# A sixth block's layer ahead of the second MLP's turn, an output evicted amid the gates' choice, and the experts' weights split sooner

## Chip, core and metric

The kernel runs on one core of one Trainium2 chip. The metric is the device time of one execution in microseconds (us); lower is better. Times of single instructions come from one profiled execution and are counted from the start of its span.

## What is computed

The reference is one block of a gated cross-attention model on `x` of 16 x 256 tokens with 256 features. Cut to what matters:

```
ref_xattn(z, x):
  zn    = layernorm(z @ W_in + b_in)                  # 16 x 120 context tokens
  h     = silu(pe @ Wp1 + bp1) @ Wp2 + bp2            # a filter, times a window
  dcwhz = causal_convolution(zn, window * h)[every second step]
  xr    = x + silu(layernorm(x) @ W1a + b1a) @ W1b + b1b        # first MLP
  y     = xr * dcwhz
  return y + silu(layernorm(y) @ W2a + b2a) @ W2b + b2b         # second MLP

ref_ffn(x):                                            # 8 heads of 32, 16 experts, 2 chosen
  t      = (x @ Wm + bm) split into heads of 32
  w      = softmax(t @ expert_emb); top two of 16, lowest index first on ties
  hmid   = gelu(t @ W1[e] + b1[e])                     # all 16 experts, 128 wide
  eo     = hmid @ W2[e] + b2[e]
  return (sum over the chosen of w * eo) @ Wo + bo

x = x + tanh(g_xattn) * ref_xattn(ctx, layernorm(x))
x = x + tanh(g_ffn)   * ref_ffn(layernorm(x))
```

The output is 4096 rows of 256 in float32. The kernel gets its accuracy by splitting most matmul operands in a high and a low part and adding three products (hi x hi, lo x hi, hi x lo).

## The kernel before

The 4096 tokens are cut in eight blocks of 512 (`NB`, `TB`). A block is a job of three kinds: `Mlp1` (first MLP, `jobs[0..7]`), `Mlp2` (second MLP, `mlp20`, `mlp21`, `mlps[2..7]`) and `Route` (choice of the experts, `route0`, `routes[1..7]`). Each job has the same steps. `norms` finds the roots of the variances on VectorE (ten tiny instructions, lines 146 to 165, and an offset, L175). `prep` normalises (L184 on ScalarE, L188 on VectorE). `turn` transposes on TensorE (L235), copies the high part out of PSUM on ScalarE (L237) and the low part on VectorE (L238). `first` is a layer with four groups of six matmuls (L205), each followed by two ScalarE activations (L259, L260) and a subtraction on VectorE or GpSimd (L268). `second` is a layer of 48 matmuls (L278), and its output is evicted by VectorE (L884 for the first MLP, L361 for the second, followed there by the statistics L170 and L171).

The program has three stages. In the first some 157 us the first MLP's blocks 0 to 4 are interleaved with the convolution. Then comes the stage that the change touches, "behind the convolution", from 157 us to some 250 us. There blocks 5 to 7 of the first MLP, blocks 0 and 1 of the second MLP and the choice of block 0 are brought up to the point where the third stage can begin. The third stage is a loop of 256 steps, one for each block, half of the heads and expert. A step has four matmuls `hps` (L1273), two Gelu activations on ScalarE (L1278), four matmuls `eo` (L1288), a VectorE product with the gates (L1296) and a GpSimd sum (L1298). The remaining MLPs and choices ride along in the loop at steps that `begun` names (`layer`, `split_laid`, `heads`, `logits`).

From line 965 on, the order of the instructions on each engine is the order in which the Python code issues them (`tc.manual_schedule()`); nothing reorders them. Generators are what interleaves work: `whole(gen)` issues all that is left of a job's step, `some(gen, n)` the next n pieces of it. Each engine takes its queue in order, so an instruction that waits holds up everything behind it on that engine, and SyncE's DMA queue is likewise in order.

Buffers set further waits. PSUM has the pools `turn`, `first`, `second` and `conv`, two banks each; `last_bank` hands out those of `conv`. `first` on a third group needs the bank of the first group back, and so the ScalarE activations that read it. `second` needs two banks at once. The staging tiles of the late weights (`stage`) have two buffers.

`late_weights` is a generator that loads and splits the weights of the third stage. `halves` splits one weight in two parts, the high part on ScalarE (L999) and the low part on GpSimd (L1000). Before the change it goes: load `Wm` and the embeddings; split them; load both halves of the experts' `W1` and `b1`, and `W2`; split both halves of `W1` (L1048 on ScalarE, L1049 on GpSimd); load `Wo`; split `Wo`. `some(weights)` at certain places of the stage takes one step of it.

`choose` is the gates' choice on VectorE: transpose (L436), maximum (L449), difference (L452), exponential on ScalarE (L458), sum and reciprocal (L461, L463), a GpSimd product (L464), then a chain of eight compare and reduce steps (L468 to L481), two GpSimd products (L482, L483) and a transpose (L488). It yields after most steps, and the loop over `route0.second(last_bank)` puts a piece of `behind_it()` after each.

Of the kernel before, what the change touches and what calls it, by code (L numbers as in the profile page):

```python
# [24 lines left out]
FP = mybir.dt.float32  # L25
# [8 lines left out]
P = 128  # L34
# [59 lines left out]
def block_kernel(  # L94
# [445 lines left out]
    with ExitStack() as ph:  # L540
# [476 lines left out]
        def late_weights():  # L1017


            t_wm = staged(Wm.rearrange("(c p) n -> p c n", p=P), 2, D, nc.sync)  # L1020
            t = first_p.tile([P, 4 * D], FP, name="stage", tag="stage", bufs=2)
            t = t.rearrange("p (q c) -> p q c", c=P)[:, 0:2]
            nc.gpsimd.memset(t, 0.0)
            for q in range(2):
                for g in range(4):
                    nc.sync.dma_start(t[bass.ts(g, HD), q, bass.ts(4 * q + g, E)], emb)
            yield
            halves(wm, t_wm)
            halves(bd, t)
            yield  # L1030
            ts = []
            for q in range(2):
                ee = slice(8 * q, 8 * q + 8)
                t = first_p.tile([P, 4 * D], FP, name="stage", tag="stage", bufs=2)
                t = t.rearrange("p (e i) -> p e i", i=I)[0:KST]
                for g in range(3):
                    nc.sync.dma_start(t[bass.ts(g, HD)], W1[ee].rearrange("e h i -> h e i"))
                for k in range(2):
                    nc.sync.dma_start(
                        t[3 * HD + k : 3 * HD + k + 1], b1[ee].unsqueeze(0)  # L1040
                    )
                ts.append((wst[0:KST, ee], t))
            nc.sync.dma_start(w2s, W2.rearrange("e i o -> i e o"))
            yield

            low = slice(2 * HD, 3 * HD + 1)
            for w, t in ts:
                nc.scalar.copy(w, t)  # L1048
                nc.gpsimd.tensor_tensor(w[low], t[low], w[low].bitcast(FP), ALU.subtract)  # L1049
            yield  # L1050
            t = staged(Wo.rearrange("(c p) n -> p c n", p=P), 2, D, nc.sync)
            yield
            halves(wo, t)
            yield
# [85 lines left out]
        jobs[5].prep()  # L1140
        some(weights)
        whole(turn(mlp20, last_bank, place))
        whole(turn(jobs[5], bank))
        some(weights)
        ahead = jobs[5].first(bank)
        mlp21.stats()
        whole(mlp20.first(last_bank))
        mlps[2].stats()
        some(ahead, 2)
        mlp21.norms(mlps[2])  # L1150
# [3 lines left out]
        for t in stacks[:2]:  # L1154
            units(t)
        whole(ahead)
        route0.norms()
# [23 lines left out]
        def behind_it():  # L1181
# [4 lines left out]
            yield from mlp21.second(bank)  # L1186
            yield from jobs[6].first(bank)
            free.append(place)
# [6 lines left out]
            lay(a)  # L1195
            some(weights)
            yield
# [8 lines left out]
            nc.scalar.activation(gelu, cv[:, 0:1], AF.Gelu)  # L1206
            some(weights)
            for _ in jobs[7].second(bank):
# [13 lines left out]
        for n, _ in enumerate(route0.second(last_bank)):  # L1222
            if n == 0:
                load_stacks(0, route0.td)
                some(rest)
            some(rest)
        while not free:
# [11 lines left out]
    with ExitStack() as ph:  # L1239
# [389 lines left out]
```

## Time and profile before

| | |
|---|---|
| median of 3 runs | 937.1 us (934.39 to 937.55) |
| profiled execution, whole time | 936.37 us |
| its span, first to last instruction | 934.6 us |
| TensorE (PE) busy | 897.2 us, 96% of the span |
| VectorE (DVE) busy | 707.2 us, 76% |
| ScalarE (ACT) busy | 673.2 us, 72% |
| GpSimd (POOL) busy | 565.6 us, 61% |
| 157 to 250 us: PE, DVE, ACT, POOL busy | 85.5, 70.6, 62.7, 47.9 of 93.0 us |
| mean granted TensorE clock | 0.987 |

Busy shares are averages over stages with different limits, so a change in one stage is read from that stage's own waits. "PEld" is the loading of weights, which lies beside the matmuls. "PEclk" is the share of the TensorE clock that was granted in a stretch: 1.00 is full speed, 0.50 half. A row of a timeline gives start, duration, engine, line, operation, tiles and shape, and in brackets the idle time of the engine before it and what ended that.

### The profile page before, as it was taken

The page shows a single profiled execution, that of the slowest core. Times are in us where ns is not written, and L with a number is a line of the kernel's source. Part 1 is how long each engine was busy: PE and PEld are TensorE (multiplying, and loading weights), DVE is VectorE, ACT ScalarE, POOL GpSimd, SP SyncE. Part 2 cuts the span into 40 slices and gives each one's busy share as a digit, 9 for nine tenths or more (in the row PEclk, how much of TensorE's full clock was granted, in tenths as well). Part 3 has the DMA queues.
Part 4 walks back from the last instruction along what each step waited for, and adds up shares of the span by engine and source line. Part 5 has one row for each costly group of instructions (what it writes and reads, how often), then busy time and mean ns, then how long its engine had stood idle before and what let it go on. Part 6 is the DMA issues. An engine that isn't in the chain of part 4 may idle for free.

```text
span 934.6 us, 16793 instructions
## 1 busy us (share of the span) xinstructions
PE 897.2 (96%) x6070; PEld 485.9 (52%) x6070; DVE 707.2 (76%) x1304; ACT 673.2 (72%) x862; POOL 565.6 (61%) x456
## 2 busy tenths in 40 slices
PE   5999998999889999999999999999999999989996
PEld 2777777887434445444454445444545434433333
DVE  5886548776778988998799789879985984783343
ACT  3544445686678788778778887887787777877883
POOL 4222123446568767777777867777767757585553
PEclk9999999999899999999999999999999999999997
DMA  7668970444439466846765694678566756836441
GB/s 244 171 201 219 217 175 24 94 114 124 135 99 228 127 175 191 196 141 160 216 162 141 186 235 118 168 198 198 151 163 191 166 141 169 215 94 177 124 124 46
DMA packets 88296, 149.89 MB, mean 160 GB/s; under 512 B 10250, under 2 KB 51722, under 8 KB 88206
## 3 DMA queue, kind: packets, MB, share of 16 engines
q1 hardware_dynamic: 85428, 141.08, 57.6%
q0 software_dynamic: 1808, 6.69, 2.3%
q10 hardware_dynamic: 976, 1.05, 0.4%
q8 instruction: 48, 0.79, 0.4%
q14 instruction: 36, 0.29, 0.1%
HBM read 120.32 MB, written 28.46 MB: 159 GB/s over the span
## 4 chain that ended last, share of the span: by engine, by line
PE 60%; DVE 20%; DMA 8%; issue 6%; POOL 2%; ACT 2%; SPq 2%; POOLq 0%; DVEq 0%; ACTq 0%
PE hps L1273 19%; PE eo L1288 17%; DVE part L1296 5%; PE aux L1332 5%; DMA gates<-g_d 4%; PE b_first L205 4%; PE b_second L278 3%; PE b_conv L908 2%; PE aux L205 2%; DMA hk<-filt_d 2%; DMA t_d<-t_lo 1%; PE b_conv L205 1%; DVE ex L371 1%; DVE d L481 1%; PE b_conv L724 1%
## 5 line engine op out<-in xcount | busy, mean ns | idle before, releaser
L1278 ACT ACTIVATE hid<-hps 128x1024 f32<-128x1024 f32 x512 | 512.4, 1026 | 139.6 <-PE hps L1273 126.1
L1298 POOL TENSOR_TENSOR comb<-comb,part 128x512 f32<-128x512 f32 x240 | 329.7, 1374 | 159.7 <-DVE part L1296 154.0
L1273 PE MATMUL hps<-stack,wst 98*128 98x512 f32 x1024 | 342.4, 426 | 4.6 <-ACT hid L1278 4.6
L1273 PEld LDWEIGHTS hps<-stack,wst 98*128 98x128 f32 x1024 | 162.9, 189 | 249.7 <-ACT hid L1278 120.0
L1288 PE MATMUL eo<-hid,w2s 128*32 128x512 f32 x2048 | 274.1, 607 | 7.8 <-DVE part L1296 7.3
L1296 DVE SCALAR_TENSOR_TENSOR part<-eo,cv,gates 128x512 f32<-128x512 f32 x237 | 175.5, 744 | 90.6 <-PE eo L1288 68.2
L1288 PEld LDWEIGHTS eo<-hid,w2s 128*32 128x32 f32 x2048 | 40.6, 108 | 102.9 <-issue 47.2
L268 POOL TENSOR_TENSOR s_lo<-silu,s_hi 128x512 fp32r<-128x512 f32 x16 | 20.4, 1287 | 68.5 <-ACT silu L260 54.8
L1391 POOL TENSOR_TENSOR s_lo<-silu,s_hi 128x512 fp32r<-128x512 f32 x24 | 31.0, 1293 | 33.6 <-DVE s_hi L1390 27.0
L1389 DVE SCALAR_TENSOR_TENSOR silu<-silu,u 128x512 f32<-128x512 f32 x24 | 26.1, 1086 | 22.6 <-ACT u L1386 22.6
L1423 DVE TENSOR_SCALAR n<-Y,mv,r_r 128x256 f32<-128x256 f32 x44 | 37.2, 887 | 3.0 <-POOL nt_lo L1447 3.0
L259 ACT ACTIVATE s_hi<-b_first,b1f 128x512 fp32r<-128x512 f32 x32 | 22.0, 686 | 22.5 <-PE b_first L205 21.8
L278 PE MATMUL b_second<-v_hi,s_hi 128*128 128x256 f32 x144 | 37.3, 292 | 0.0
L278 PE MATMUL b_second<-v_lo,s_hi 128*128 128x256 f32 x144 | 36.0, 283 | 0.0
L1447 POOL TENSOR_TENSOR nt_lo<-n,nt_hi 128x512 fp32r<-128x512 f32 x26 | 33.6, 1292 | 3.0 <-PE hps L1273 2.6
L908 PE MATMUL b_conv<-hk,zn 60*32 60x256 f32 x1024 | 31.8, 378 | 0.0
L915 ACT COPY cvs<-b_conv 128x256 f32<-128x256 f32 x32 | 10.5, 375 | 27.5 <-PE b_conv L908 27.4
L278 PEld LDWEIGHTS b_second<-v_hi,s_hi 128*128 128x128 f32 x144 | 27.6, 191 | 3.3 <-issue 2.8
L1446 DVE CAST nt_hi<-n 128x512 fp32r<-128x512 f32 x26 | 28.2, 1084 | 0.0
L1471 POOL TENSOR_TENSOR Y<-Y,tbo 128x256 f32<-128x256 f32 x28 | 28.0, 1011 | 0.0
L278 PEld LDWEIGHTS b_second<-v_lo,s_hi 128*128 128x128 f32 x144 | 27.6, 192 | 0.4
L205 PE MATMUL b_first<-nt_hi,w_hi 128*128 128x512 f32 x64 | 27.2, 426 | 0.6 <-ACT silu L260 0.6
(284 smaller groups left out, 1480.2 us busy)
## 6 DMA issues: line engine op xcount, KB each, us to landing
gates<-g_d SPq DMA_DIRECT2D x126, 512.0 KB
hk<-filt_d SPq DMA_DIRECT2D x128, 134.1 KB
stack<-t_d SPq DMA_DIRECT2D x48, 256.0 KB
g_d<-gt SPq DMA_DIRECT2D x32, 256.0 KB
n<-laid_d SPq DMA_DIRECT2D x13, 512.0 KB
laid_d<-laid SPq DMA_DIRECT2D x44, 128.0 KB
xr<-in_x SPq DMA_DIRECT2D x8, 512.0 KB
t_d<-t_hi SPq DMA_DIRECT2D x16, 256.0 KB
```

Of the source, the lines that this page charges most:

```text
L205: nc.tensor.matmul(out=out, lhsT=l, rhs=r, start=(i == 0 and j == 0), stop=(i == n - 1 and j == 2),)
L278: nc.tensor.matmul(out=ps[:, j, :], lhsT=s[k][l][:, c], rhs=v[r][:, k], start=(k == 0 and i == 0 and not (whole and (j or bias))), stop=(k ...
L908: nc.tensor.matmul(out=ps[bass.ts(c, 2 * B), 0:L], lhsT=zn[rows, 4 * n + c, k, e * B : (e + 2) * B], rhs=hk[rows, 2 * c + e, k * SQ : k * ...
L1273: nc.tensor.matmul(out=ps[:, g, :], lhsT=wst[0:KST, e, :], rhs=st[0:KST, 2 * g2 + g, :], start=True, stop=True,)
L1278: nc.scalar.activation(t, ps, AF.Gelu)
L1288: nc.tensor.matmul(out=eo[bass.ts(g, HD)], lhsT=w2s[:, e, :], rhs=hid[g // 2][:, g % 2, :], start=True, stop=True,)
L1296: nc.vector.scalar_tensor_tensor(to, eo, col("b2", e), gs, ALU.add, ALU.mult)
L1298: nc.gpsimd.tensor_tensor(comb, comb, to, ALU.add)
L1332: nc.tensor.matmul(out=ps, lhsT=w[l][:, k, c], rhs=r[:, k], start=(k == 0 and j == 0), stop=(k == 1 and j == 2),)
L1391: nc.gpsimd.tensor_tensor(lo, f, hi.bitcast(FP), ALU.subtract)
L1423: nc.vector.tensor_scalar(job.n[:, j + k, :], Y[:, t0 + k, :], mv[:, t0 + k, 0:1], job.r[:, j + k : j + k + 1], ALU.subtract, ALU.mult,)
L1447: nc.gpsimd.tensor_tensor(lo, src, hi.bitcast(FP), ALU.subtract)
```

## The change

It moves work within the stage behind the convolution and shifts some pieces of the loop's first block; no arithmetic is added or removed.

1. **The sixth block's layer.** `turn(jobs[5])` and the first two groups of `jobs[5].first` are issued ahead of `turn(mlp20)`. Before, both turns came first, and these two groups stood between `mlp20.first` and `mlp20.second`.
2. **Weights.** `Wo` is loaded together with the first half of the experts' `W1`, in place of the second half, and split in the middle of the stage. The second half of `W1` is loaded after that. The first half of `W1` is split between the second and third group of `jobs[6].first`, the second half after `jobs[7].first`. The splits at the stage's end go away.
3. **The output amid the choice.** After each of the first three yields of `route0.second` one more piece of `behind_it()` is issued (three, two and two in place of two, one and one). The eviction of `mlp21.second` (L361, with its statistics) so comes after the fifth compare step (L472) and not after the last (L481).
4. **The loop's first block.** The pieces of `layer(m)` go from steps 2, 2, 3, 3, 4, 4, 5, 5 to 2, 3, 4, 4, 5, 5, 6, 7; `split_laid(a)`, `heads` and `logits` come one step later.

```diff
@@ late_weights
-            ts = []
-            for q in range(2):
+            def experts(q):
...
-                ts.append((wst[0:KST, ee], t))
-            nc.sync.dma_start(w2s, W2.rearrange("e i o -> i e o"))
-            yield
-
-            low = slice(2 * HD, 3 * HD + 1)
-            for w, t in ts:
+                return wst[0:KST, ee], t
+
+            def experts_split(w, t):
+
+                low = slice(2 * HD, 3 * HD + 1)
                 nc.scalar.copy(w, t)
                 nc.gpsimd.tensor_tensor(w[low], t[low], w[low].bitcast(FP), ALU.subtract)
-            yield
-            t = staged(Wo.rearrange("(c p) n -> p c n", p=P), 2, D, nc.sync)
-            yield
-            halves(wo, t)
+
+            t_wo = staged(Wo.rearrange("(c p) n -> p c n", p=P), 2, D, nc.sync)
+            some_experts = experts(0)
+            nc.sync.dma_start(w2s, W2.rearrange("e i o -> i e o"))
+            yield
+            halves(wo, t_wo)
+            t = experts(1)
+            yield
+            experts_split(*some_experts)
+            yield
+            experts_split(*t)
             yield
@@ behind the convolution
         some(weights)
+        whole(turn(jobs[5], bank))
+        ahead = jobs[5].first(bank)
+        some(ahead, 2)
         whole(turn(mlp20, last_bank, place))
-        whole(turn(jobs[5], bank))
         some(weights)
-        ahead = jobs[5].first(bank)
         mlp21.stats()
         whole(mlp20.first(last_bank))
         mlps[2].stats()
-        some(ahead, 2)
...
         for t in stacks[:2]:
             units(t)
+        some(weights)
         whole(ahead)
@@ behind_it
-            yield from jobs[6].first(bank)
+            soon = jobs[6].first(bank)
+            for n, _ in enumerate(soon):
+                if n == 1:
+                    some(weights)
+                yield
...
             lay(a)
-            some(weights)
             yield
...
             nc.scalar.activation(gelu, cv[:, 0:1], AF.Gelu)
-            some(weights)
@@ loop over route0.second
-            some(rest)
+            some(rest, 2 if n < 3 else 1)
@@ begun, i == 0
-                at = {"split": 6, "heads": range(8, 12), "logits": (12, 13)}
+                at = {"split": 7, "heads": range(9, 13), "logits": (13, 14)}
-                yield sorted(2 * (2, 3, 4, 5)), layer(m)
+                yield (2, 3, 4, 4, 5, 5, 6, 7), layer(m)
```

More of the change, by code (lines that the diff above doesn't have):

```diff
@@ L1041, in late_weights @@
                     )
-                ts.append((wst[0:KST, ee], t))
+                return wst[0:KST, ee], t
+            def experts_split(w, t):
+                low = slice(2 * HD, 3 * HD + 1)
+                nc.scalar.copy(w, t)
+                nc.gpsimd.tensor_tensor(w[low], t[low], w[low].bitcast(FP), ALU.subtract)
+            t_wo = staged(Wo.rearrange("(c p) n -> p c n", p=P), 2, D, nc.sync)
+            some_experts = experts(0)
             nc.sync.dma_start(w2s, W2.rearrange("e i o -> i e o"))
             yield
-            low = slice(2 * HD, 3 * HD + 1)
-            for w, t in ts:
-                nc.scalar.copy(w, t)
-                nc.gpsimd.tensor_tensor(w[low], t[low], w[low].bitcast(FP), ALU.subtract)
+            halves(wo, t_wo)
+            t = experts(1)
             yield
-            t = staged(Wo.rearrange("(c p) n -> p c n", p=P), 2, D, nc.sync)
+            experts_split(*some_experts)
             yield
-            halves(wo, t)
+            experts_split(*t)
             yield
```

## Prediction

> **What bounds the kernel now.** I read the page first. TensorE is busy 96% of the span and leads the chain of waits; the change removes no matmul, so only idle time of PE and time at a low clock can be won or lost.
>
> ```profile
> PE   5999998999889999999999999999999999989996
> PEclk9999999999899999999999999999999999999997
> PE 60%; DVE 20%; DMA 8%; issue 6%; POOL 2%; ACT 2%; SPq 2%; POOLq 0%; DVEq 0%; ACTq 0%
> ```
>
> One slice in mid-kernel has a dip in both rows: the tenth on, from 234 us, the end of the stage that is changed. PE's timeline names the stalls there:
>
> ```profile
> 157.82 1.74 PE L235 MATMUL b_conv<-ident,n 128*128 128x128 f32 x8 [0.77 <-DVE n L188]
> 162.00 0.73 PE L205 MATMUL b_conv<-stack,w_hi 128*128 128x512 f32 x2 [1.57 <-DVE stack L238]
> ...
> 212.06 0.50 PE L293 MATMUL b_second<-b_in,pick 64*128 64x512 f32 x1 [0.70 <-DVE Y L361]
> 213.90 0.49 PE L293 MATMUL b_second<-b_in,pick 64*128 64x512 f32 x1 [1.34 <-DVE Y L361]
> ...
> 237.40 0.73 PE L1273 MATMUL hps<-stack,wst 98*128 98x512 f32 x2 [2.69 <-ACT hid L1278]
> ```
>
> They add up to 7.07 us, and all three places are edited. Between them PE has no gap over 0.3 us. The table by stretches shows what a stall costs afterwards (length, PE busy, PEld, DVE, ACT, POOL, clock, DMA):
>
> ```profile
> 159.60:163.00 3.40, 1.83 (x12) 1.46 (x11) 3.40 (x6) 1.61 (x4) 2.77 (x2) 1.00 0.00 0
> 210.80:214.20 3.40, 1.35 (x5) 0.49 (x3) 3.26 (x8) 0.00 (x0) 2.70 (x3) 1.00 0.00 0
> 214.20:217.60 3.40, 3.40 (x15) 3.19 (x15) 2.76 (x7) 1.93 (x3) 2.30 (x2) 0.51 0.11 13
> 234.70:238.10 3.40, 0.71 (x3) 0.30 (x2) 3.23 (x14) 2.02 (x3) 1.26 (x1) 1.00 0.46 109
> 238.20:241.60 3.40, 3.28 (x12) 1.20 (x12) 3.26 (x11) 2.96 (x4) 2.37 (x2) 0.50 0.38 116
> 241.60:245.00 3.40, 3.40 (x12) 1.36 (x12) 2.32 (x8) 1.47 (x2) 0.77 (x2) 0.50 0.76 225
> ```
>
> A stretch of 3.4 us in which PE works 1.35 or 0.71 us is followed by one or two at half clock; 1.83 us of work had no such sequel, 1.60 us (920.7 to 924.1) had. The limit is near 1.7 us of idle time in a stretch, and a slow stretch full of work costs 1.7 us. Three slow stretches cost the stage up to 5.1 us.
>
> The last view is the timelines of the helpers, for who is late:
>
> ```profile
> 161.27 1.28 DVE L238 TENSOR_TENSOR stack<-b_conv,stack 128x512 fp32r<-128x512 f32 x2
> 211.42 1.27 POOL L482 TENSOR_TENSOR one<-one,d 128x512 f32<-128x512 f32 x1 [5.43 <-DVE d L481]
> 212.76 1.27 POOL L483 TENSOR_TENSOR ex<-ex,one 128x512 f32<-128x512 f32 x1
> 220.04 2.08 ACT L184 ACTIVATE n<-Y,off,r_r 128x256 f32<-128x256 f32 x4 [2.82 <-DVE off L175]
> 236.33 2.87 ACT L1278 ACTIVATE hid<-hps 128x1024 f32<-128x1024 f32 x3 [1.38 <-POOL wo_lo L1000]
> 156.17 0.16 DVE L158 TENSOR_TENSOR r_t<-r_t,r_ve 128x4 f32<-128x4 f32 x1
> 256.86 1.21 DVE L158 TENSOR_TENSOR r_t<-r_t,r_ve 128x20 f32<-128x20 f32 x1
> ```
>
> **The front, 157 us on: a loss of 5.5 us.** PE can now start the sixth block's transposes at 157.05 (its `n` was written by 154.2), so the wait of 0.77 goes. But PE resumes when the first low part is written, and VectorE still has `n` (157.36), `xr` and `xb` ahead of it: the first L238 stands at 161.27, 0.69 us long, as before. PE starts real work at 162.0, as before, with only eight of sixteen transposes done. From there, at full clock: eleven matmuls at 0.233 us to 164.6, `mlp20`'s transposes to 165.5; ScalarE has four activations (0.575 us apart) ahead of the copy of the high part, which ends at 166.5, L238 at 167.2, so PE idles 1.5 us. Then `mlp20.first` to 173.0. `mlp20.second`, which had twelve matmuls of cover ahead of it, now needs at once the banks of the last two groups; the last activation waits for GpSimd's four subtractions (1.27 us each from 168.2) and ends at 174.0: 0.5 us idle. It ends at 179.3; before, the same work was done at 176.9. Loss 2.4 us. Nothing absorbs it: up to 212 PE has no slack.
>
> The clock adds to this. PE is idle from 158.6 to 162.0 but for one matmul; 3.4 us cannot be laid over two stretches without leaving 1.7 in one, and by the old phase 2.3 fall into the second. That slows the next stretch: 4.3 us of loss. The wait for ScalarE then comes at 167.2 to 169.0, some 1.8 us, which may slow one more: 6.0. I take 5.5, since an idle 1.8 is on the slow side of the rows above; the ends are 2.4 and 6.0.
>
> [...]
>
> **The choice: 1.3 us later.** The stalls of 0.70 and 1.34 and the slow stretch after them go, since L361 now precedes five steps of the chain. But VectorE's chain then ends later, and that decides when PE goes on: route 1's `norms` stand behind it, its four normalisations (220.04) are in ScalarE's queue ahead of the activations that free the first bank of `jobs[7].first` at 223.28, and PE took its third group at 224.27. Now the last compare, L481, ends at 211.34 + 3.71 (the evictions and statistics, 211.26 to 214.97) + c. The two GpSimd products, 2.62 us, are no longer covered by the evictions; only two L268 lie beside them. With L488 (0.68) and the roots (2.15) `off` is there at 220.6 + c against 220.0. For c: two L268 on GpSimd (1.27 each) and the split of the first half of `W1` (2.38) now run amid the chain. The last two rows show a VectorE step with two SBUF inputs, 0.16 us alone, 1.21 while GpSimd adds (`comb` from 256.74 to 258.03). Five compare steps and two L268 are of that kind; two or three such meetings cost 1.7, none 0, five 5. So `off` comes 2.2 later, the bank at 225.5 and the third group 1.3 us later than before. The ends are c = 0, bank at 223.9, 0.4 us earlier than before, and c = 5, 4.6 later.
>
> [...]
>
> Without the old stalls PE is ready for that group 9.1 us of work after 211.4, at 220.5, and idles 5 us. Between a half and two stretches of slow clock must follow, as 2.69 us of idle were followed by 6.8 us: 2.5 us (0.9 to 3.4), on `jobs[7]`'s dense matmuls.
>
> **The start of the loop: 4.6 us won.** From the first `hps` (233.63) to the third `eo` (246.72) it took 13.1 us. Its 18 matmuls `hps` (0.277 each, two in 0.55) and two groups `eo` (0.99) are 7.0 us at full speed, and the first Gelus, 1.03 each, hold PE up some 1.5: 8.5 us. `Wo`'s late load, its 5.7 us to landing (from 228.62) and its split no longer stand ahead of the Gelus. The later split of `W1` does, 1.0 on ScalarE (half of 2.00), covered by `jobs[7].second`'s 6.4 us; its 2.38 on GpSimd is needed only by the ninth expert. Ends 3 and 5.5.
>
> **The loop's first block: +1 us.** The shifted pieces meet rows with stalls of 1.75 (ACT, 266.55) and 0.63 (POOL `nt_lo`, 270.05); the first should shrink, the second grow, because the split and the last activation's subtraction now fall in the same two steps of GpSimd. From -1 to +3.5. DMAs that moved (`Wo`, `W1`, 128 to 256 KB each) have tens of microseconds to land; SyncE's queue waits for `Wo`'s split before `t_d`, which is due later. Both cost nothing; were `t_d` late, the loads of the stacks still have 30 us.
>
> **Sum.** 5.5 + 1.3 + 2.5 - 4.6 + 1.0 = +5.7. The profiled execution took 936.4 us (span 934.6), 0.7 under the median of 937.1; 5.7 on both gives 942.1 and 942.8, and I say 942.5. All low ends together give -3.6, all high ends +14.5.
>
> **Rivals.** *The clock holds*: the new gaps, at the front and in `jobs[7].first`, are not followed by slow stretches. Then the front costs 2.4, the 2.5 goes, and 2.4 + 1.3 + 0 - 4.6 + 1.0 = +0.1: 937.2, not slower, and with the choice or the loop at their low ends 934.5. It is decided at 1.7 us of idle time in a stretch. For it speaks that 1.57 us did no harm at 159.6; against it that the gaps are 3.4 and 5 us. Chance 0.22, 0.10 of it faster, 0.12 the same. *The loop loses too*: two stalls fall into one stretch between steps 8 and 12 and slow the next two, +3.4, some 946. Chance 0.15. *`Wo` was not what held the Gelus*: the second split of `W1` takes its place ahead of them, so the start of the loop wins 1 instead of 4.6: 946. The row at 236.33 names `wo_lo`; chance 0.07. The forecast itself has 0.56, of which 0.04 lie within 0.3% and 0.02 below.
>
> Some 0.3% (2.8 us) is what a measurement can tell from no change. Faster 0.12, same 0.16, slower 0.72. The range, 934.5 to 949.5, leaves a tenth out on either side.
>
> **What would show it.** In the changed profile: PE idle some 3.4 us before 162 and slow after it; a stall before `mlp20.first`; no stall by L361; a stall of 4 to 6 us in `jobs[7].first`, ended by ScalarE; no stall and full clock at the first Gelus. The prediction is wrong if the stall in `jobs[7].first` is under 2 us, or the front stays at full clock.

## The result, and the profile after

The changed kernel takes 938.05 us (median of 20 runs, 936.15 to 941.44), the kernel before in the same rounds 935.67 us (20 runs, 932.38 to 937.55). The ratio is 1.0033 with a 95% interval of 1.0023 to 1.0043: 3.1 us slower, 2.2 to 4.0. The forecast was 5.4 us, from a median of three runs that lies 1.4 us above that of the twenty. The direction was right and the size 1.7 times too large (2.3 times by the two medians, which are 2.4 us apart). The profiled execution took 938.54 us, its span is 936.8.

The page of the changed kernel, PE's and the clock's slices and the chain of waits:

```profile
PE   5999998897999999999999999999999999989997
PEclk9999999999999999999999999999999999999999
PE 55%; DVE 22%; issue 9%; DMA 7%; POOL 3%; ACT 3%; SPq 1%; POOLq 0%; DVEq 0%; ACTq 0%
```

A slice is 23.4 us. PE's eighth and tenth (164 to 187 and 211 to 234 us) fell from 9 to 8 and 7, its eleventh and twelfth rose from 8 to 9, and the clock's dip in the eleventh (from 234 us; the prediction counts it as the tenth) is gone: the idle time has moved ahead. The chain has 2% more of VectorE and 5% less of PE. PE's timeline, its stalls over 0.6 us from 157 us to 280 us:

```profile
161.24 0.56 PE L205 MATMUL b_first<-nt_lo,w_hi 128*128 128x512 f32 x1 [3.12 <-DVE nt_lo L238]
...
168.23 0.73 PE L205 MATMUL b_conv<-stack,w_hi 128*128 128x512 f32 x2 [1.74 <-DVE stack L238]
...
175.66 0.39 PE L278 MATMUL b_conv<-v_hi,stack 128*128 128x256 f32 x1 [0.65 <-ACT silu L260]
...
230.28 0.79 PE L205 MATMUL b_first<-nt_hi,w_hi 128*128 128x512 f32 x1 [5.45 <-ACT silu L260]
...
242.81 0.73 PE L1282 MATMUL hps<-stack,wst 98*128 98x512 f32 x2 [0.70 <-ACT hid L1287]
...
277.42 0.50 PE L1341 MATMUL aux<-nt_lo,wm_hi 128*128 128x512 f32 x1 [1.19 <-POOL nt_lo L1456]
```

The two stalls by L361 are gone and the one at the first Gelus is 0.70 in place of 2.69. New are 3.12 and 0.65 at the front and 5.45 in `jobs[7].first`; 1.74 stands where 1.57 stood. The table by stretches (length, PE, PEld, DVE, ACT, POOL, clock, DMA):

```profile
158.11:161.53 3.42, 0.30 (x2) 0.29 (x2) 3.42 (x6) 0.00 (x0) 2.06 (x1) 1.00 0.00 0
161.53:164.94 3.41, 3.41 (x9) 2.68 (x9) 0.25 (x1) 1.26 (x2) 3.11 (x4) 0.50 0.02 5
164.94:168.35 3.41, 1.67 (x12) 1.25 (x11) 0.87 (x2) 2.23 (x4) 3.39 (x4) 1.00 0.54 155
...
226.39:229.80 3.41, 0.00 (x0) 0.00 (x0) 2.51 (x8) 2.79 (x6) 0.00 (x0) 1.00 0.49 139
229.80:233.22 3.42, 2.94 (x7) 2.37 (x8) 1.80 (x3) 3.09 (x7) 2.92 (x3) 0.50 0.44 162
233.22:236.63 3.41, 3.41 (x19) 2.50 (x19) 1.64 (x4) 3.41 (x7) 2.09 (x2) 1.00 0.50 131
```

Each of the two large stalls is followed by one slow stretch. The stretch from 164.94, in which PE idles 1.74 us, is followed by full clock. L477 in the kernel before, and the helpers' timelines amid the choice after the change:

```profile
208.47 0.69 DVE L477 TENSOR_TENSOR c<-d,top 128x512 f32<-128x512 f32 x1
```

```profile
216.49 2.06 DVE L477 TENSOR_TENSOR c<-d,top 128x512 f32<-128x512 f32 x1
220.64 2.40 DVE L268 TENSOR_TENSOR s_lo<-silu,s_hi 128x512 fp32r<-128x512 f32 x2
...
215.26 2.73 POOL L1048 TENSOR_TENSOR wst<-stage,wst 33x1024 fp32r<-33x1024 f32 x1
220.87 1.62 POOL L482 TENSOR_TENSOR one<-one,d 128x512 f32<-128x512 f32 x1 [2.87 <-DVE d L481]
222.56 1.63 POOL L483 TENSOR_TENSOR ex<-ex,one 128x512 f32<-128x512 f32 x1
...
227.01 2.07 ACT L184 ACTIVATE n<-Y,off,r_r 128x256 f32<-128x256 f32 x4 [9.93 <-DVE off L175]
```

L477, 0.69 us before, takes 2.06 beside GpSimd's split of `W1`, and ScalarE stands 9.93 us for the offset that ends VectorE's chain, with the activations that PE waits for behind it: the matmuls whose output they read ended at 219.2 and 222.0 us, and they start at 228.99. In the trace the chain from L468 to L481 has nine steps, and the eviction stands behind the third (L472), with six behind it: "eight", "fifth" and "five" in the texts ahead are miscounts, the lines that they name are right.

### The profile page after: what moved, and what is told of

It is laid out like the page before. It is cut to its first block, busy times and chain, and to the rows that moved or that the text cites. A ratio compares the mean times of both kernels' runs of the same rounds, so it can differ in the third digit from the quotient of the medians.

```text
span 936.8 us, 16799 instructions
## 1 busy us (share of the span) xinstructions
PE 894.5 (95%) x6070; PEld 484.5 (52%) x6070; DVE 706.4 (75%) x1304; ACT 672.2 (72%) x862; POOL 565.8 (60%) x456
## 4 chain that ended last, share of the span: by engine, by line
PE 55%; DVE 22%; issue 9%; DMA 7%; POOL 3%; ACT 3%; SPq 1%; POOLq 0%; DVEq 0%; ACTq 0%
PE hps L1282 18%; PE eo L1297 16%; DVE part L1305 6%; PE aux L1341 5%; PE b_first L205 3%; PE b_conv L908 3%; PE b_second L278 3%; DMA gates<-g_d 3%; DMA t_d<-t_lo 2%; PE aux L205 2%; PE b_conv L205 1%; DMA hk<-filt_d 1%; DVE d L481 1%; ACT hid L1287 1%; DVE ex L371 1%
## 5 line engine op out<-in xcount | busy, mean ns | idle before, releaser
L268 POOL TENSOR_TENSOR s_lo<-silu,s_hi 128x512 fp32r<-128x512 f32 x16 | 20.4, 1282 | 67.6 <-ACT silu L260 53.8
L205 PE MATMUL b_first<-nt_lo,w_hi 128*128 128x512 f32 x64 | 27.2, 425 | 3.8 <-DVE nt_lo L238 3.8
```

Source lines behind the costliest of these rows:

```text
L205: nc.tensor.matmul(out=out, lhsT=l, rhs=r, start=(i == 0 and j == 0), stop=(i == n - 1 and j == 2),)
```

## The experiments

Fifteen variants and two clock probes were run. The first part of the program, up to 157 us, is the same in all but ended between 156.1 and 159.3 us in the profiles, so the table counts from the start of the second MLP's `n` on VectorE (157.36 before, 156.81 after). This `n` starts 0.3 us behind the last matmul of `jobs[4].second`; in e7 and e15, which move `n` itself, the table counts from 0.3 us behind that matmul. It gives the difference to before at the first matmul with `Wm`, the third group of `jobs[7].first`, the first `hps`, the third `eo` and step 20 of the loop. Then come PE's idle time and the slow stretches (3.41 us at half clock) from 156 to 300 us, summed from the traces, and the ratio to the kernel before, run alongside. e11 and e13 hold the changed kernel unaltered up to its end, so they are two more profiles of it.

| kernel | `Wm` | third group | first `hps` | third `eo` | step 20 | idle | slow | ratio |
|---|---|---|---|---|---|---|---|---|
| before | 0 | 0 | 0 | 0 | 0 | 9.8 | 3 | |
| after | +4.7 | +6.6 | +7.9 | +3.6 | +3.4 | 14.5 | 2 | 1.0033 (1.0023 to 1.0043) |
| e11, same | +4.8 | +6.6 | +8.1 | +3.7 | +3.5 | 14.6 | 2 | |
| e13, same | +4.8 | +6.6 | +9.3 | +6.5 | +6.2 | 15.3 | 4 | |
| e1 front alone | +4.1 | +5.7 | +5.7 | +4.4 | +5.3 | 11.8 | 5 | 1.0070 (1.0047 to 1.0092) |
| e2 weights alone | -0.2 | +0.7 | +0.8 | -0.5 | -0.5 | 8.7 | 3 | 0.9993 (0.9982 to 1.0004) |
| e3 eviction alone | -0.2 | +0.2 | +1.8 | +3.9 | +3.9 | 13.3 | 4 | 1.0050 (1.0037 to 1.0063) |
| e4 loop alone | -0.2 | +1.3 | +1.2 | +1.5 | +1.2 | 9.5 | 4 | 1.0012 (0.9998 to 1.0026) |
| e5 no front | -0.2 | +1.6 | +3.9 | +2.4 | +3.6 | 11.0 | 5 | 0.9995 (0.9979 to 1.0011) |
| e6 no eviction | +4.6 | +5.6 | +7.2 | +4.3 | +4.0 | 13.0 | 3 | 1.0054 (1.0034 to 1.0075) |
| e7 front early | +1.8 | +3.6 | +5.3 | +0.9 | +0.7 | 12.9 | 2 | 1.0014 (0.9994 to 1.0033) |
| e8 | +5.5 | +1.7 | +4.9 | +7.5 | +8.7 | 14.0 | 7 | 1.0078 (1.0051 to 1.0104) |
| e9 | +4.4 | +0.5 | +7.7 | +6.5 | +7.7 | 13.2 | 6 | 1.0073 (1.0060 to 1.0086) |
| e10 | +4.2 | +6.4 | +8.4 | +4.0 | +3.8 | 14.4 | 3 | 1.0070 (1.0051 to 1.0090) |
| e12 | -0.2 | -4.0 | +2.0 | -1.1 | -1.3 | 11.1 | 1 | 1.0005 (0.9994 to 1.0017) |
| e14 | -0.2 | -4.1 | -2.2 | +0.8 | +2.0 | 11.4 | 4 | 1.0000 (0.9985 to 1.0016) |
| e15 | +3.1 | -0.6 | +1.4 | +3.8 | +3.6 | 13.4 | 3 | 1.0032 (1.0018 to 1.0046) |
| e16 | +3.0 | -0.9 | +1.0 | -1.8 | -2.1 | 9.3 | 1 | 1.0008 (0.9994 to 1.0022) |
| e17 | -0.3 | -4.0 | -2.1 | -4.9 | -5.2 | 7.0 | 1 | 0.9960 (0.9941 to 0.9979) |

### The four parts alone, on the kernel before

**e1, the front.**

```diff
-        whole(turn(mlp20, last_bank, place))
         whole(turn(jobs[5], bank))
+        ahead = jobs[5].first(bank)
+        some(ahead, 2)
+        whole(turn(mlp20, last_bank, place))
```

> The kernel before with the first part of the change alone (the sixth block's turn and two groups ahead of the second MLP's turn). Theory A, the delays add up and nothing behind takes them back: PE waits some 3.1 us for the first low part (L238), one slow stretch follows, the first matmul with Wm comes 4.2 to 4.8 us later than before (188.2), and the whole takes 4 to 5 us more. Theory B, the front's delay is slack that the gates' choice has anyway: the first matmul with Wm is as late as in A, but the third group of jobs[7].first (224.3 before) moves by less than 2 us and the whole takes less than 2 us more.

The stall is 3.12 again, one slow stretch follows, and 4.1 us at `Wm` have become 5.3 at step 20. Theory A: nothing up to there gives the delay back. The runs give more than was expected, 6.5 us (4.4 to 8.6).

**e2, the weights** (`Wo` loaded and split sooner, the halves of `W1` apart).

```diff
+            t_wo = staged(Wo.rearrange("(c p) n -> p c n", p=P), 2, D, nc.sync)
+            some_experts = experts(0)
...
+            halves(wo, t_wo)
+            t = experts(1)
```

> The kernel before with the second part alone (Wo loaded and split sooner, the two halves of W1 split apart). Here the first half of W1 is split behind the choice's two products on GpSimd, not amid the choice. Theory A, Wo's late split is what held the first Gelus: from the first hps to the third eo it takes 8.7 us in place of 13.1, no slow stretch stands there, the whole takes 4 to 5 us less. Theory B, that stretch was short in the changed kernel only because PE came to it later with everything else ready: here it takes 11 us or more, and the whole 0 to 2 us less.

```profile
237.13 0.73 PE L1282 MATMUL hps<-stack,wst 98*128 98x512 f32 x2 [0.70 <-ACT hid L1287]
```

The figures are those of theory B, its reason is not. The stall at the first Gelu, 2.69 before, falls to 0.70, as in the changed kernel, with this part alone: `Wo`'s late split was what held the Gelus. But from the first `hps` to the third `eo` it takes 11.8 us (8.7 after, 13.1 before): PE's three short waits there (0.70, 0.18, 0.20) fell into one stretch, and two slow ones followed, as many as before. So 3.1 of the 4.4 us that lie between 13.1 and 8.7 hang on the clock. The whole is no faster that can be told.

**e3, the eviction amid the choice.**

```diff
-            some(rest)
+            some(rest, 2 if n < 3 else 1)
```

> The kernel before with the third part alone (the second MLP's output evicted after the fifth compare step). Theory A, the choice's last steps decide: the stalls of 0.70 and 1.34 us by L361 and the slow stretch behind them go, but the third group of jobs[7].first comes 0.5 to 2 us later than before (224.3) after an idle time of some 4 to 5 us, with one or two slow stretches behind it: 1 to 4 us more in all. Without W1's split amid the choice L477 takes its 0.7 us, so the whole is 1 us or more better than the change's share in the changed kernel (third group +1.8, clock +1.4). Theory B, PE's work is what counts and the eviction sooner frees it: 1 to 4 us less.

Theory A on the choice (L361's stalls go, 4.20 of idle time in `jobs[7].first` come), but the third group is only 0.2 later, and the loss arises behind it. Here, where no split of `W1` stands amid the choice, L477 takes 0.69 us and the third group comes 0.5 later counted from `Wm`; in e5, with the split, L477 takes 2.06 and the third group comes 1.8 later. So 1.4 of the choice's 1.8 us in the changed kernel are the split's. ScalarE's timeline at the first Gelus:

```profile
238.57 0.62 ACT L999 CAST wo_hi<-stage 128x512 fp32r<-128x512 f32 x1 [3.96 <-DMA stage<-in_Wo]
240.56 1.94 ACT L1278 ACTIVATE hid<-hps 128x1024 f32<-128x1024 f32 x2 [1.37 <-POOL wo_lo L1000]
```

`Wo`'s load needs a staging buffer that `W1`'s split gives back, and stands in SyncE's queue behind the four writes of a normalised tile, the last of which ends just before it (233.53 and 233.58); which of the two holds it is not shown. Both come behind the choice, so load, split and first Gelu come later, PE waits 3.75 us and three slow stretches follow. With the part on the weights beside it the stall is 0.70 again (e5). So the parts are no sum: alone they come to 0.70 - 0.07 + 0.50 + 0.12 = 1.25%, together to 0.33%.

**e4, the loop's first block.**

```diff
-                yield sorted(2 * (2, 3, 4, 5)), layer(m)
+                yield (2, 3, 4, 4, 5, 5, 6, 7), layer(m)
```

> The kernel before with the fourth part alone (the pieces in the loop's first block shifted). Theory A, the shift only moves short stalls about: the whole within 0.7 us of before. Theory B, as forecast, split and subtraction meet in GpSimd's queue and two stalls fall in one stretch: 1 us more or above. Theory C, the shift takes the stall of 1.75 us by ScalarE at step 10 away: 1 to 2 us less.

Theory A in the trace: from the third `eo` to step 20 it takes 0.2 us less than before. The runs (1.0012) leave it open. PE's stalls there, in the kernel before and in the changed one:

```profile
266.55 0.73 PE L1273 MATMUL hps<-stack,wst 98*128 98x512 f32 x2 [1.75 <-ACT hid L1278]
270.05 0.50 PE L1332 MATMUL aux<-nt_lo,wm_hi 128*128 128x512 f32 x1 [0.63 <-POOL nt_lo L1447]
```

```profile
273.39 0.72 PE L1282 MATMUL hps<-stack,wst 98*128 98x512 f32 x2 [0.34 <-ACT hid L1287]
277.42 0.50 PE L1341 MATMUL aux<-nt_lo,wm_hi 128*128 128x512 f32 x1 [1.19 <-POOL nt_lo L1456]
278.85 1.06 PE L1297 MATMUL eo<-hid,w2s 128*32 128x512 f32 x8 [0.48 <-DVE part L1305]
```

### The two stalls, undone and mended

**e5, the changed kernel without the first part** (the diff of e1 the other way round).

> The changed kernel with the first part undone (the sixth block's turn and groups stand where they stood). Theory A, the front's delay is carried unshortened to the end: the first matmul with Wm comes at some 188 in place of 192.4, and the whole is 4 to 5.5 us under the changed kernel, 1.5 to 3 us under the one before. Theory B, the parts are no sum (alone they came to far more than together): the idle time in jobs[7].first or the first Gelus grow as the front shrinks, and the whole is less than 2 us under the changed kernel.

Theory A in kind: the stalls of 5.45 and 0.70 stay as they were and the front's delay is gone, so the ratio is 0.0038 under the changed kernel's, 3.6 us. That is short of the 4 to 5.5 expected, and it is not faster than the kernel before.

**e6, without the third part** (the diff of e3 the other way round).

> The changed kernel with the third part undone (the output is evicted behind the last compare step again, so W1's split no longer stands amid the choice either). Theory A, VectorE's chain decides when PE goes on: the stalls of 0.70 and 1.34 by L361 are back, the one in jobs[7].first falls from 5.45 to under 1 us, and the third group comes 1 to 2 us sooner than in the changed kernel; the whole is 1 to 3 us under it. Theory B, the eviction pays once the weights are split sooner (it took the first Gelus' wait away): the whole is the same as the changed kernel's or over it.

The stalls moved as in A (0.71 and 1.34 back, 5.45 down to 1.93, the third group 0.9 us sooner), the whole did not: 1.0054, above the changed kernel. At step 20 the two traces are 0.7 us apart. A's gain failed; whether the eviction pays, as in B, the overlapping intervals leave open.

**e7, VectorE's order at the front.**

```diff
-        mlp20.prep()
...
-        mlp20.stream()
         whole(jobs[4].second(bank))
...
         whole(turn(jobs[5], bank))
+        mlp20.prep()
+        mlp20.stream()
         ahead = jobs[5].first(bank)
```

> The changed kernel with the second MLP's normalisation and its product xr on VectorE moved behind the sixth block's turn, so that the low parts (L238) stand directly behind the two evictions xb. Theory A, the front loses because PE waits for VectorE's queue: the wait of 3.12 us falls below 1, the slow stretch at 161.5 goes, the stall of 1.74 behind it stays, the first matmul with Wm comes at some 188 to 188.5 in place of 192.4, and the whole is 3.5 to 4.5 us under the changed kernel. Theory B, the loss comes from the second layer standing directly behind its first one (banks and GpSimd's subtractions): PE only waits later, the first matmul with Wm comes at 190.5 or later, and the whole is less than 2 us under.

```profile
158.53 0.50 PE L205 MATMUL b_first<-nt_lo,w_hi 128*128 128x512 f32 x1 [0.58 <-DVE nt_lo L238]
...
163.19 0.77 PE L235 MATMUL b_conv<-ident,n 128*128 128x128 f32 x5 [1.49 <-DVE n L188]
164.98 0.73 PE L205 MATMUL b_conv<-stack,w_hi 128*128 128x512 f32 x2 [1.03 <-DVE stack L238]
```

The first row stood at 3.12 of idle time, and the slow stretch behind it is gone: theory A on the cause of that stall. But `n` comes later now, its four instructions take 4.14 us in place of 1.38, and PE waits 1.49 for them and 1.03 for the low part. At `Wm` the front still costs 1.8 us, 2.9 less than in the changed kernel; at step 20 it is 2.6 less. The runs give 1.8 us (1.0014 against 1.0033), as theory B has it for the whole. So VectorE's queue was the cause of some three fifths of the front's loss, and this order hands the rest on.

**e8, the normalisations behind all of `jobs[7].first`.**

```diff
-            a.prep()
             rest, soon = jobs[6].second(bank), jobs[7].first(bank)
...
+            a.prep()
+            lay(a)
+            m.prep()
             some(weights)
             lay(m)
```

> The changed kernel with route 1's and the third MLP block's normalisations on ScalarE (and what follows from them) moved behind all four groups of jobs[7].first. Theory A, the idle 5.45 us are there only because four normalisations that wait for VectorE's chain stand in ScalarE's queue ahead of the activations that free the bank: the idle time goes, the third group comes at some 224.5 in place of 230.3, no slow stretch follows, the first hps comes at 234 to 236 in place of 241.0, and the whole is 4 to 6 us under the changed kernel. Theory B, VectorE's chain is needed anyway: PE waits as long in jobs[7].second for the low parts or at the first Gelus for the normalisations, and the whole is less than 2 us under.

Theory B. The 5.45 are gone and the first `hps` comes 3.0 us sooner, but the offset (L175) now stands behind low parts and statistics on VectorE. PE waits 4.62 us at the first Gelu, three slow stretches follow: 1.0078.

**e9, the offset early again, `a.prep()` after two groups.**

```diff
             for gen in (rest, soon, rest, soon, rest):
                 yield next(gen)
+            a.prep()
             lay(a)
```

> The changed kernel with route 1's normalisations on ScalarE behind the activations of the first two groups of jobs[7].first alone (its roots and offset stay where they are on VectorE), and the third block's behind those of the last two groups. Theory A, in e8 the idle time came back at the first Gelu because VectorE had the offset (L175) behind two low parts and four statistics; with the offset early nothing is late: the stall of 5.45 falls below 1 us, the first hps comes at 235.5 to 237.5 in place of 241.0, the stalls at the first Gelus are under 1.5 us together, and the whole is 3 to 5 us under the changed kernel. Theory B, the first Gelu cannot come sooner whatever the order: the stall there grows to 3 us or more, and the whole is less than 2 us under.

```profile
231.17 1.39 PE L293 MATMUL b_second<-b_in,pick 64*128 64x512 f32 x2 [4.21 <-DVE xb L884]
```

Neither theory: the third group comes 6 us sooner, and PE stands 4.21 us in `jobs[7].second`, because VectorE has the eviction `xb` behind the transposes L522, which wait for `n`. The wait was handed on to the next queue.

**e10, `W1`'s first half split behind the choice's products.**

```diff
-                if n == 1:
-                    some(weights)
                 yield
             free.append(place)
+            some(weights)
```

> The changed kernel with the first half of W1 split behind all four groups of jobs[6].first, so that GpSimd does it behind the choice's two products (L482, L483) and not amid the chain. Theory A, GpSimd's split is what stretched VectorE's steps and pushed the products back (L477 2.06 us, two L268 2.40): L477 takes 0.7 us, the pair 1.3, the offset comes 2 to 2.7 us sooner than in the changed kernel, the stall of 5.45 in jobs[7].first falls to some 3 us, one slow stretch still follows, and the whole is 1.5 to 3 us under. Theory B, the eviction's own steps in the chain are the delay: the offset moves by less than 1 us and the whole is the same.

VectorE's and GpSimd's timelines:

```profile
216.38 0.69 DVE L477 TENSOR_TENSOR c<-d,top 128x512 f32<-128x512 f32 x1
...
223.38 1.83 DVE L146 TENSOR_SCALAR r_ve<-mv 128x4 f32<-128x4 f32 x1
...
222.79 2.40 POOL L1048 TENSOR_TENSOR wst<-stage,wst 33x1024 fp32r<-33x1024 f32 x1
```

L477 is back at 0.69 and the chain ends 1.9 us sooner, 0.5 of which the front of this profile had won already, so the split is what stretched it. But now the split runs beside the roots, L146 takes 1.83 in place of 0.13, and the offset is only 0.2 us sooner (from `Wm`, 0.4 later). Theory A holds for L477 and fails for the offset; the two L268 stay at 2.38, beside the choice's products on GpSimd. The whole is no better (1.0070 against 1.0033).

### The clock

**e11, a probe with dense matmuls** behind the changed kernel's end.

```diff
+                for q in range(60):
+                    nc.tensor.matmul(out=ps, lhsT=wo[0][:, 0, 0:P], rhs=wm[0], start=q == 0, stop=q == 59)
+                nc.scalar.copy(wm[1][:, 0, 0 : g[0]], ps[:, 0 : g[0]])
+                for w in g[1:]:
+                    nc.scalar.copy(...)
```

> The changed kernel, and behind its end 52 blocks of sixty dense matmuls of 128x512 (some 14 us each), parted by idle times of PE of some 0.6 to 4 us, each of thirteen sizes four times (a short chain of ScalarE copies holds PE up). Its time is longer by the added work. Theory A, the clock falls when some 1.4 to 1.7 us of a stretch of 3.41 us are idle: gaps under 1.2 us are never followed by a slow stretch, gaps over 3 us always, and those between sometimes, by how they lie over two stretches; what follows is one slow stretch, two where the gap fills most of one. Theory B, a whole stretch has to be idle: no gap under 3.4 us is followed by one. Theory C, the idle time of a gap alone decides: the same size always gives the same answer.

The gaps came out in thirteen sizes from 0.37 to 2.77 us. PE's timeline, and the stretches of the clock's own grid around a gap of 2.12 and one of 2.77:

```profile
1114.09 15.49 PE L1582 MATMUL aux<-wm_hi,wo_hi 128*128 128x512 f32 x60 [2.12 <-ACT wm_hi L1585]
1132.36 0.96 PE L1582 MATMUL aux<-wm_hi,wo_hi 128*128 128x512 f32 x3 [2.77 <-ACT wm_hi L1585]
```

```profile
1110.99:1114.41 3.42, 1.30 (x6) 0.78 (x5) 0.00 (x0) 1.96 (x4) 0.00 (x0) 1.00 0.00 0
1114.41:1117.82 3.41, 3.41 (x9) 2.64 (x8) 0.00 (x0) 0.00 (x0) 0.00 (x0) 0.50 0.02 5
1128.06:1131.48 3.42, 1.53 (x7) 0.94 (x5) 0.00 (x0) 1.79 (x4) 0.00 (x0) 1.00 0.00 0
1131.48:1134.89 3.41, 2.53 (x11) 2.12 (x12) 0.00 (x0) 0.79 (x2) 0.00 (x0) 1.00 0.00 0
```

The gap of 2.12 lies within one stretch, all of it or all but 0.15, and the next is slow (four times of four). That of 2.77 lies over two, 1.89 and 0.88, and nothing follows (three of three). 1.91 us within a stretch were followed by a slow one; the same gap split in two (three times) was not. Up to 1.47 us never were. So theory A's form is right, with a limit between 1.89 and 1.91 us of a stretch among these matmuls. Theory C falls. So does B, which asks for a whole stretch of 3.41 us: 1.91 us of one sufficed.

**e13, a probe with the loop's matmuls.**

```diff
+            for kind in ("hps", "eo", "mix"):
+                for g in gaps:
...
+                    if kind == "hps":
+                        hps_block(ps, 56)
+                    elif kind == "eo":
+                        eo_block(eo, 28)
```

> The changed kernel, and behind its end 54 blocks of some 14 us with the loop's own matmuls (hps alone, eo alone, both in turn as in the loop), parted by idle times of PE of some 0.5 to 2.5 us, each of six sizes three times for each kind. Its time is longer by the added work. Theory A, the limit is the same 1.9 us of a stretch as with the dense matmuls of e11, and the slow stretches that the loop's start showed after 1.1 to 1.5 us have another cause: no gap under 1.9 is followed by one. Theory B, these matmuls fill the array less and count for less: gaps of 1.2 to 1.5 us within one stretch suffice with at least one of the kinds, and a kind that fills too little goes at half clock without any gap.

```profile
1358.32:1361.73 3.41, 1.88 (x9) 1.24 (x8) 0.00 (x0) 1.32 (x5) 0.00 (x0) 1.00 0.00 0
1361.73:1365.15 3.42, 3.42 (x9) 2.66 (x9) 0.00 (x0) 0.00 (x0) 0.00 (x0) 0.50 0.00 0
```

Theory B for one kind, as far as the gaps go; its reason is not shown. Among `hps` alone (98 of 128 rows), 1.53 us in a stretch were enough, 1.19 were not. Among `eo` alone 1.78 were not, and in the mixture 1.62 were not and 2.32 were. No kind went slow without a gap (from 1150 to 1153.4 us, full of `eo`, the granted clock was 1.00). At the start of the loop itself even 1.02 to 1.09 us were followed by a slow stretch (e2, e5, e6, e13's own, e16, e17) while 0.88 (e7, e10), 1.12 (e1), 1.20 (e4) and 1.60 (e12) were not; the probe did not reproduce that, and it stays open.

### Can the stall behind the choice be had at all?

**e12, e9's order without the front.** The diffs of e5 and e9 together.

> The changed kernel with its first part undone (as in e5) and ScalarE's normalisations as in e9. Theory A, the two losses of the changed kernel are the front and the stall in jobs[7].first, and both add up: 3 to 5 us under e5, some 930 to 932, 4 to 6 under the kernel before. Theory B, the first Gelu holds the gain back: within 1.5 us of e5.

The trace has 4.06 us before L293 and 2.03 at the first Gelu. At step 20 it is 1.3 us ahead of before; the runs show no difference, from before or from e5. That is theory B's figure, with most of the wait one place ahead of the Gelu.

**e14, evictions and both offsets ahead on VectorE, all normalisations last on ScalarE.**

```diff
             yield from rest
+            a.norms()
+            a.off = offset(mv3[:, 4 * a.i : 4 * a.i + 4, 0], a.r, 4)
+            m.off = offset(mv2[:, 4 * m.i : 4 * m.i + 4, 0], m.r, 4)
             for _ in soon:
...
             some(weights)
+            a.prep()
+            lay(a)
+            m.prep()
             lay(m)
```

> The changed kernel with its first part undone, and behind the choice VectorE evicts jobs[6].second ahead of route 1's roots, both offsets come directly behind them, ScalarE normalises behind all activations of jobs[7].first and the second split of W1. Theory A, each of e8, e9 and e12 only moved the wait to the next queue (ScalarE's offset, then VectorE's xb behind the transposes L522); with all of them behind what PE needs, PE waits less than 2 us between jobs[7].first and the first eo in all, the first hps comes 4 to 6 us sooner than in e12 (235.0, counted from a start of the stage at 156.8), and the whole is 4 to 6 us under the kernel before, some 930. Theory B, the chain that ends with the gates or VectorE's statistics holds the loop's first product anyway: the first eo comes less than 2 us sooner than in e12 (240.6), and the whole is within 2 us of the kernel before.

```profile
236.62 2.14 PE L1288 MATMUL hps<-stack,wst 98*128 98x512 f32 x4 [5.26 <-ACT hid L1293]
```

Theory B. The first `hps` comes 4.1 us sooner than in e12, counted from the same start, and PE then stands 5.26 us for the first Gelu, since ScalarE's second normalisation waits for VectorE's transposes. **e15, the same with e7's front:**

> As e14, but with the sixth block's layer ahead, as changed, and the second MLP's normalisation and xr behind its turn, as in e7. Theory A: the front costs nothing against the kernel before (e7 had -0.6 us at the first matmul with Wm), so the whole is the same as e14's within 1 us. Theory B, a stall in that front falls in one stretch with another and slows it: 1.5 us or more over e14.

Theory B: two stalls of its front (1.48 and 1.03) fell into one stretch, and a slow one followed; 1.0032 against e14's 1.0000. That e7's front had cost nothing, on which theory A rests, was a misreading: -0.6 us was counted from the moved `n`, and it is +1.8. e15 is 3.1 us late at `Wm` and e14 is not, and the runs are 3.0 us apart.

**e16, work taken out of VectorE's queue:** twelve of sixteen statistics moved ahead, the third block's normalisation moved into the choice.

```diff
         mlps[2].stats()
+        some(stats_3, 4)
...
         mlp21.stream()
+        some(stats_3, 2)
...
+                if n == 3:
+                    mlps[2].prep()
+                    lay(mlps[2])
```

> As e14 (front undone, evictions and offsets ahead), and twelve of VectorE's sixteen statistics of the later blocks (0.55 us each, 6.6 in all) moved from the stage's end into its idle times at 164 and 192 us, and the third block's normalisation and transposes into the choice. Theory A, VectorE's queue behind the choice is what the wait is handed along: with 8 us less in it the first Gelu waits under 1.5 us in place of 5.26, the first eo comes 4 us or more sooner than in e14, and the whole is 4 to 7 us under the kernel before. Theory B, the wait only goes on to the loop's first products and layers: the first eo comes sooner, but step 20 is within 2 us of e14's, and the whole is within 2 us of the kernel before.

The first Gelu waits 0.71 us, as in A. But eight statistics stood on VectorE behind the low parts of `mlp20.first`, where it has no idle time, and 3.0 us went at `Wm`. **e17, these eight put into VectorE's idle 4.3 us:**

```diff
         mlp21.stats()
+        some(stats_3, 4)
         whole(mlp20.first(last_bank))
         mlps[2].stats()
-        some(stats_3, 4)
```

> As e16, with the eight statistics of the fourth and fifth block put ahead of the low parts of mlp20.first, into VectorE's idle 4.3 us, where e16 put them behind these and so had the first matmul with Wm 3.0 us later than before. Theory A, that misplacement was all that e16 lacked: the first matmul with Wm comes within 0.5 us of before's, the first Gelu still waits under 1.5 us, step 20 comes 4 us or more sooner than before, and the whole is 3 to 6 us under the kernel before. Theory B, the statistics delay the low parts of mlp20.first (a wait of 1 us or more in mlp20.second): step 20 is within 2.5 us of before's and the whole within 2 us.

```profile
161.81 0.72 PE L205 MATMUL b_conv<-stack,w_hi 128*128 128x512 f32 x2 [1.35 <-DVE stack L238]
...
229.32 0.74 PE L278 MATMUL b_second<-v_hi,s_lo 128*128 128x256 f32 x4 [1.45 <-DVE s_lo L268]
...
233.34 0.73 PE L1293 MATMUL hps<-stack,wst 98*128 98x512 f32 x2 [0.70 <-ACT hid L1298]
```

Theory A: 931.0 us against 934.7 (medians of 12 and 17 runs), 3.7 us under the kernel before, ratio 0.9960 (0.9941 to 0.9979). With that it is ahead of both kernels, by 0.4% of the one before. No stall over 1.5 us is left from 157 us on to step 20, and one slow stretch stands there. It keeps the second, third and fourth part of the change and drops the first. Against e14 it moves three things, the statistics and the third block's offset and normalisation; what each of them is worth is not shown, only that the place of eight statistics is worth the step from 1.0008 (e16).

## Why the prediction was right in direction and wrong in size

**What bounds it** was read rightly: PE's idle time in this stage and what the clock does after it. Every stall forecast came, at its place: 3.12 us at the front (3.4 forecast), 1.74 (1.8) and 0.65 (0.5) behind it, none by L361, 5.45 in `jobs[7].first` (5), ended by ScalarE. What failed are sizes in the sum: in all three executions the loop's first block (+1.0 forecast, -0.2 measured) and the front (5.5, 4.7 to 4.8), and in two of three the clock's price behind the idle time (2.5, 1.4 and 1.5). The terms, with the three executions of the changed program (after, e11, e13):

- *The front*, 5.5 forecast: 4.7, 4.8, 4.8. The lost 2.4 and one slow stretch came (4.3 in the forecast's own sum); the second slow stretch, for which it added 1.2, did not. The mis-sized step is the limit: 1.7 us of idle time, read from rows of two kinds of work. Among dense matmuls it lies between 1.89 and 1.91 (e11), and the stall left 1.74. e7 shows that VectorE's queue was the cause of the large stall; 1.8 us of the loss stay without it.
- *The choice*, 1.3: 1.8 in all three. c was right in kind (L477, in e3, e5 and e10) and low in size: on the way to the offset L477 lost 1.4, and the two GpSimd products, priced at 2.62, took 3.32, together 2.1 against 1.7. The pair of L268, 2.40 long, lies beside the products. What the traces show of the meeting are its sizes (L477 2.06 us beside the split, 0.69 without it in e3 and e10); what in the hardware makes them is not shown.
- *The clock behind the idle time*, 2.5 (0.9 to 3.4): 1.4, 1.5, 2.7. One stretch or two, by how 5.45 us lie on the grid: behind the idle stretch up to 0.5 us of idle time were left in the first two of these, 0.97 in e13. The same stall was followed by two stretches in e5, e7 and e10 as well. The mean of one and a half was a fair price, and the profile drew the cheap side: the low figure is luck.
- *The start of the loop*, -4.6: -4.4, -4.4, -2.9. `Wo` was what stood ahead of the Gelus (e2's row: 2.69 down to 0.70), so that rival falls. Full clock there, worth 3.1 of the 4.4 (e2), was taken as sure and is not: in e13 the same waits were followed by a slow stretch, in e2 by two.
- *The loop's first block*, +1.0: -0.2 in all three. Which stall shrinks and which grows was right (1.75 to 0.34, 0.63 to 1.19, and 0.48 new behind it), but idle time did not grow in sum. The term is -0.2 to -0.3 where no slow stretch comes and +1.1 to +1.3 where one does, which was 4 of 15 profiles with this part (e5, e8, e9, e14). The step that failed took as the rule what is the exception: a slow stretch behind these stalls. The rival "the loop loses too" came only as that exception, with one slow stretch and not two, and +1.2 in place of +3.4.
- *Behind step 20*, 0: -0.6 in the profiled execution, by where the last slow stretches fell.

So 5.7 became 2.75 in the profiled execution, counted from the start of the stage: -0.8 + 0.5 - 1.1 + 0.25 - 1.2 - 0.6. Of the two others, e11 stood at +3.5 at step 20 and e13 at +6.2, over the forecast. PE's idle time came out nearly the same in the three (14.5, 14.6 and 15.3 us), the number of slow stretches did not (2, 2 and 4). The rival "the clock holds" is false as a whole, as slow stretches followed both large stalls, and right for the front's second. The rest of the gap to the median is the base: the forecast was laid on a median of three runs that stood 1.4 us high.

## What to carry to other kernels

Price a stall as its own length and, apart from it, a slow stretch by the chance that enough of it falls within one interval of the clock's grid (3.41 us in these traces; 1.91 idle in one were enough among dense matmuls in e11, 1.53 among `hps` in e13). One profile shows one draw: 2, 2 and 4 slow stretches in three executions here. Before moving a matmul ahead, look at what its low part waits for on the helper's queue (3.12 us here), not only at when its input is written. And where a helper's queue was full, another order only handed the wait on, four times here (4.62 us in e8, 4.21 in e9, 4.06 in e12, 5.26 in e14); taking work out of that queue, into its own idle times elsewhere, came with the only gain (3.7 us, e17).

## What was not expected of the hardware

A longer idle time was cheaper than a shorter one: after 2.77 us over two stretches the granted clock stayed at 1.00, after 1.91 within one it was 0.50 for 3.41 us (e11). Among matmuls on 98 of 128 rows the limit lay lower, between 1.19 and 1.53 us (e13); that the rows are the reason is not shown. And a VectorE instruction of 128x4 elements, 0.13 us, took 1.83 beside a GpSimd subtraction (e10; it reads one tile, so the two inputs of the prediction's rows are not what it takes), so a tiny step of the chain was stretched there as a large one was (L477, 128x512, 0.69 to 2.06).
